# Last layer: two source blocks at a time, count rows on four row groups, clamps on two engines

## The chip, the cores and the metric

The kernel runs on one core of a Trainium2 chip. A core has a matrix engine (TensorE, PE in the profile, with its weight loads shown as PEld), three engines for elementwise work (VectorE or DVE, ScalarE or ACT, GpSimd or POOL), a queue for data movement (SyncE or SP), an on-chip memory of 128 partitions, and eight PSUM banks of 512 fp32 values a partition, into which TensorE accumulates. The metric is the time of one execution in microseconds (us).

## The reference

Four graph layers follow each other on 4096 nodes with 64 features, all over the same 4096 x 4096 adjacency matrix; each is preceded by a layer norm with a maximum at zero, and adds its result to the nodes. The change is in the last layer (and in the end of the third, which prepares an operand for it):

```python
support = input @ weight
mask = (adj != 0).astype(support.dtype)
rank = jnp.cumsum(mask, axis=1)
deg = rank[:, -1:]
k = jnp.minimum(deg, float(MAX_NEIGH))  # 100
pos = rank - (deg - k)
w = mask * jnp.where(pos > 0, DECAY ** (k - pos), 0.0)  # DECAY = 0.5
out = w @ support + bias
```

So an edge from a source column weighs 0.5 to the power of the number of edges to its right in the same row, and nothing if there are 100 or more of these.

## The kernel before

**Layout.** Sources stand in 32 blocks of 128 (NB = 32, index j), on the partitions. Destinations stand on the free axis, in groups of 512 (G), which is one PSUM bank. The transposed edge mask lies in device memory as one byte an edge and is loaded by SyncE in pieces of four source blocks (`m`, L2747, JT = 4, NQ = 8 pieces).

**The weight as a number's bits.** The kernel never computes a power. It builds, in PSUM, 128 x (100 - number of later edges) where there is an edge and something not positive where there is none or too many are later; clamped at zero and written as a 16-bit integer, this is the bit pattern of a bf16 power of two (128 is one step of its exponent). Two products make it. The triangle product (L2762) multiplies the 128 x 128 matrix `tri` with the block's mask: the diagonal gives 100 x 128 at an edge, the rest subtracts 128 for each later edge in the same block. The count-row product (L2754) adds what later blocks hold: `late` has, on 32 partitions, one count for each source block (already limited to 128), and `blk` picks row j and spreads it, times -128, over 128 partitions. It contracts over 32 partitions only, so it takes up one of TensorE's four groups of 32 rows.

**The loop.** For each quarter of the destinations (u = 0 to 3, 1024 columns, NK = 2 groups) the kernel goes over the 32 blocks. For each block: two count-row products into the two halves of one PSUM tile `pv` of two banks, two triangle products on top of these, one clamp of all 1024 columns on ScalarE (L2771) into `w3b`, and then, for the block before, two sums (L2736) of the supports `SS` times the weights into `sacc`, which are two PSUM banks held for the whole quarter. The pool `ps_v` has two `pv` tiles, four banks; `w3b` has three buffers. After the quarter the sums are copied out by ScalarE and VectorE (`ev`, L2778), turned by small products with `fold_3` (L2783), and VectorE adds the bias and the nodes (`og`, L2791 and L2792); GpSimd's queue stores the result (L2793).

**Which row groups.** `late` holds four times 32 rows for each half of the destinations, one set for each group of 512. Quarter u uses the sets (u mod 2) x 2 and the next one: two row groups at a time.

**What sets the order around it.** The layers are written as loops, and a scheduler orders the instructions of each engine ahead of time; at run time each engine goes through its own list in that order and waits on semaphores. The third layer is done in two halves of the destinations (`hf`). The groups of its second half (`layer2_group`, four serial chains over TensorE, VectorE and ScalarE: L2634, the transposes L1000, L2645, the norm, and at the end L2668 and `SS` at L2671 to L2674) therefore stand mixed with the last layer's first quarter, whose `late` is ready from the first half's end. That quarter's sums of the second half of the sources need the `SS` of these groups. At the end of each half a product (L2724) and a limit (L2725) make `late` of that half.

Of the kernel before, what the change touches and what calls it, by code (L numbers as in the profile page):

```python
# [9 lines left out]
F32 = mybir.dt.float32  # L10
BF16 = mybir.dt.bfloat16
F16 = mybir.dt.float16
F8 = mybir.dt.float8e4
I32 = mybir.dt.int32
I8 = mybir.dt.int8
I16 = mybir.dt.int16
U8 = mybir.dt.uint8
AF = mybir.ActivationFunctionType
ALU = mybir.AluOpType
AX = mybir.AxisListType  # L20
PSUM = bass.MemoryType.PSUM
# [3 lines left out]
P = 128  # L25
N = 4096
NB = N // P
D = 64
G = 512
NG = N // G  # L30
GB = G // P
JT = 4
# [803 lines left out]
def kernel(  # L836
# [24 lines left out]
    nc = tc.nc  # L861
    NH, F, O = W_sp.shape[0] + W_int.shape[0], W_sp.shape[1], W_sp.shape[2]
# [178 lines left out]
    with ExitStack() as l0:  # L1041
        lp = l0.enter_context(tc.tile_pool(name="l0", bufs=1))
# [258 lines left out]
        with ExitStack() as pa:  # L1301
            hp = pa.enter_context(tc.tile_pool(name="prep", bufs=1))
            work = pa.enter_context(tc.tile_pool(name="pwork", bufs=2))
# [47 lines left out]
            with in_order():  # L1351
                nc.vector.tensor_reduce(fsum, FT[0:F, :], AX.X, ALU.add)
                for b0 in range(0, NB, 8):
                    pw = (ps, ps2)[b0 // 8 % 2].tile([P, 8, KZ], F32, name="pst", tag="misc")
                    for b in range(8):
                        nc.tensor.matmul(
                            pw[:, b, :],
                            lhsT=FT[:, (b0 + b) * P : (b0 + b + 1) * P],
                            rhs=rhz,
                            start=True,  # L1360
                            stop=True,
# [19 lines left out]
                for g in range(HW // G):  # L1381
                    pr = (ps, ps2)[g % 2].tile([P, G], F32, name="psr", tag="misc")
                    nc.tensor.matmul(
                        pr, lhsT=srep, rhs=FT[:, g * G : (g + 1) * G], start=True, stop=True
# [27 lines left out]
                for k in range(2):  # L1412
                    pr = ps.tile([P, G], F32, name="prs", tag="misc")
                    for q in range(4):
# [3 lines left out]
                            lhsT=rs,  # L1418
                            rhs=FT[:, g * G : (g + 1) * G],
                            start=True,  # L1420
                            stop=True,
# [23 lines left out]
        with ExitStack() as ha:  # L1445
            hp = ha.enter_context(tc.tile_pool(name="heads", bufs=2))
            work = ha.enter_context(tc.tile_pool(name="hwork", bufs=1))
# [458 lines left out]
        HO2 = N // 4  # L1906
# [614 lines left out]
    def layers_fast(es, wide, *sums):  # L2521
# [75 lines left out]
        with not_before_nodes():  # L2597
# [25 lines left out]
            nc.vector.tensor_scalar(w3, w3, Q3[0:D], VAL, ALU.mult, ALU.mult)  # L2623
            fold_3 = lp.tile([P, D], F32, name="fold_3f")
            nc.vector.tensor_scalar(fold_3, fold_h, M3, 2.0**27 / VAL, ALU.mult, ALU.mult)
        late = lp.tile([P, 2, G], BF16, name="late")

        def layer2_group(b0, part, deg):

# [47 lines left out]
        with tc.tile_pool(name="ps_nacc", bufs=6, space=PSUM) as ps_acc:  # L2677
            for hf in range(2):
                accs = [ps_acc.tile([P, G], F32, name="nacc", tag="nacc") for _ in range(NS)]
                dc = ps_acc.tile([P, G], F32, name="dc", tag="nacc")  # L2680
                for q in range(NQ):
                    m = work.tile([P, JT, HW], U8, name="m2", tag="m2", bufs=3)
                    nc.sync.dma_start(m, mask_d[q][hf])
                    m8 = m.bitcast(F8)
                    for t in range(JT):
                        j = q * JT + t
                        for k in range(NS):
                            nc.tensor.matmul(  # L2688
                                accs[k],
                                lhsT=HH[:, j].rearrange("p s d -> p (s d)"),  # L2690
                                rhs=m8[:, t, k * G : (k + 1) * G],
                                start=(j == 0),
                                stop=(j == NB - 1),
                            )
                    for t in range(JT):
                        j = q * JT + t
                        for k in range(NS):
                            nc.tensor.matmul(
                                dc[k * O : (k + 1) * O, :],
                                lhsT=sel[:, j * O : (j + 1) * O],  # L2700
                                rhs=m8[:, t, k * G : (k + 1) * G],
                                start=(j == 0),
                                stop=(j == NB - 1),
                            )
                cf = work.tile([P, G], F32, name="cf", tag="cf")
                nc.vector.tensor_copy(cf, dc)
                nc.gpsimd.tensor_copy(cnt16[:, hf], cf)
                ev = work.tile([P, NS, G], F32, name="ev2", tag="ev2", bufs=1)
                for k in range(NS):
                    (nc.vector.tensor_copy if k % 2 else nc.scalar.copy)(ev[:, k, :], accs[k])  # L2710
                pd = ps.tile([P, GB, NS], F32, name="pdeg", tag="misc")
                for b in range(GB):
                    nc.tensor.matmul(  # L2713
                        pd[:, b], lhsT=cf[:, b * P : (b + 1) * P], rhs=qsel, start=True, stop=True
                    )
                deg = work.tile([P, NS, GB], F32, name="degf", tag="degf")
                nc.vector.tensor_scalar(
                    deg.rearrange("p q b -> p b q"), pd, 1.0, 1.0, ALU.add, ALU.max
                )
                nc.vector.reciprocal(deg, deg)  # L2720
                for g in range(NS):
                    layer2_group(hf * HB + g * GB, ev[:, g, :], deg[:, g, :])
                pl = ps.tile([P, G], F32, name="plate", tag="misc")
                nc.tensor.matmul(pl, lhsT=lat, rhs=cnt16[:, hf], start=True, stop=True)  # L2724
                nc.vector.tensor_scalar(late[:, hf], pl, VBITS, None, ALU.min)  # L2725


        ps_acc = es.enter_context(tc.tile_pool(name="ps_sacc", bufs=2, space=PSUM))
        ps_v = es.enter_context(tc.tile_pool(name="ps_v", bufs=2, space=PSUM))
        for u in range(4):  # L2730
            hs = slice((u % 2) * HO2, (u % 2 + 1) * HO2)
            accs = [ps_acc.tile([P, G], F32, name="sacc", tag="sacc") for _ in range(NK)]

            def add_up(j, w):
                for k in range(NK):
                    nc.tensor.matmul(  # L2736
                        accs[k],
                        lhsT=SS[:, j].rearrange("p s d -> p (s d)"),
                        rhs=w[:, k * G : (k + 1) * G].bitcast(BF16),
                        start=(j == 0),  # L2740
                        stop=(j == NB - 1),
                    )

            last = None
            for q in range(NQ):
                m = work.tile([P, JT, HO2], U8, name="m3", tag="m3", bufs=3)
                nc.sync.dma_start(m, mask_d[q][u // 2][:, :, hs])  # L2747
                for t in range(JT):
                    j = q * JT + t

                    pv = ps_v.tile([P, HO2], F32, name="pv", tag="pv")
                    for k in range(NK):
                        r = ((u % 2) * NK + k) * O
                        nc.tensor.matmul(  # L2754
                            pv[:, k * G : (k + 1) * G],
                            lhsT=blk[r : r + O, j, :],
                            rhs=late[r : r + O, u // 2, :],
                            start=True,
                            stop=False,
                        )  # L2760
                    for k in range(NK):
                        nc.tensor.matmul(  # L2762
                            pv[:, k * G : (k + 1) * G],
                            lhsT=tri,
                            rhs=m[:, t, k * G : (k + 1) * G].bitcast(F8),
                            start=False,
                            stop=True,
                        )

                    w = work.tile([P, HO2], I16, name="w3b", tag="w3b", bufs=3)  # L2770
                    nc.scalar.activation(w, pv, AF.Relu)  # L2771
                    if last is not None:
                        add_up(*last)
                    last = (j, w)
            add_up(*last)
            ev = work.tile([P, NK, G], F32, name="ev3", tag="ev3")
            for k in range(NK):
                (nc.vector.tensor_copy if k % 2 else nc.scalar.copy)(ev[:, k, :], accs[k])  # L2778
            for k in range(NK):
                b0 = (u * NK + k) * GB  # L2780
                pn = ps.tile([P, GB, D], F32, name="pn3", tag="misc")
                for b in range(GB):
                    nc.tensor.matmul(  # L2783
                        pn[:, b, :],
                        lhsT=ev[:, k, b * P : (b + 1) * P],
                        rhs=fold_3,
                        start=True,
                        stop=True,
                    )
                og = work.tile([P, GB, D], F32, name="og", tag="og")  # L2790
                nc.vector.tensor_tensor(og, pn, b3t.unsqueeze(1).to_broadcast([P, GB, D]), ALU.add)  # L2791
                nc.vector.tensor_tensor(og, og, x[:, b0 : b0 + GB, :], ALU.add)  # L2792
                nc.gpsimd.dma_start(  # L2793
                    out[b0 * P : (b0 + GB) * P, :].rearrange("(b p) f -> p b f", p=P), og
                )
# [92 lines left out]
```

## Time and profile before

| What | Value |
|---|---|
| median of 3 runs | 2041.64 us (2033.41 to 2043.93) |
| the profiled execution | 2039.13 us, of which the span from first to last instruction is 2037.1 us |
| TensorE, VectorE, ScalarE busy over the span | 89%, 75%, 72% |
| first count-row product of the last layer | at 1826.4 us |
| its four quarters end (copies `ev` start) | 1894.4, 1938.8, 1982.8, 2026.8 us |
| clamps L2771 | 128 of 1.02 us on ScalarE |

A row of a group of instructions reads: line, engine, operation, output<-input with the shapes, count, then the busy time in us and the mean of one in ns, then the idle time of its engine just ahead of it and what ended most of that. A row of the timeline reads: start, duration, engine, line, operation, and how many were merged; in brackets the idle time ahead and its releaser. A stage's row gives its bounds, its length, and each engine's busy time with the number of instructions.

### The profile page before, as it was taken

How to read it: one execution, taken by the hardware profiler on the slowest of the kernel's cores; microseconds unless marked ns; L12 is line 12 of the kernel's file. 1: busy time of each engine (PE TensorE's matmuls, PEld its weight loads, DVE VectorE, ACT ScalarE, POOL GpSimd, SP SyncE). 2: the span in 40 equal slices, each digit the busy share in tenths (PEclk: the TensorE clock that was granted, in tenths of full speed). 3: DMA queues.
4: the chain of work that ended last, by engine and by line, in shares of the span. 5: the costliest groups of instructions: out<-in, count | busy, mean ns of one | idle time of the engine just before them, and what ended most of it. 6: DMA issues, size and time to landing. Idle time of an engine off the chain costs nothing. (4 is left out here: it accounts for less than half of the span.)

```text
span 2037.1 us, 44155 instructions
## 1 busy us (share of the span) xinstructions
PE 1815.8 (89%) x19323; PEld 821.8 (40%) x19340; DVE 1530.0 (75%) x2239; ACT 1476.9 (72%) x1439; POOL 83.3 (4%) x125
## 2 busy tenths in 40 slices
PE   5889989999999999996788958999999995789998
PEld 3444445444444444443234442333333333344332
DVE  5779988998789879996989867888788788533000
ACT  2768987899689878993778847777777753227676
POOL 2000100100000000001011100000000000000000
PEclk8899999999999999997899977999999996899999
DMA  9945555434211111103686406444344334412232
GB/s 112 178 115 99 100 99 72 164 118 172 86 49 49 48 49 54 54 2 125 254 276 227 163 17 235 137 145 143 124 140 140 124 134 151 152 63 70 91 99 64
DMA packets 117016, 239.05 MB, mean 117 GB/s; under 512 B 11062, under 2 KB 84006, under 8 KB 102054
## 3 DMA queue, kind: packets, MB, share of 16 engines
q1 hardware_dynamic: 101996, 192.95, 28.1%
q0 software_dynamic: 14816, 43.18, 11.8%
q8 instruction: 153, 2.51, 0.5%
q14 instruction: 51, 0.42, 0.1%
HBM read 245.37 MB, written 49.46 MB: 145 GB/s over the span
## 5 line engine op out<-in xcount | busy, mean ns | idle before, releaser
L1205 ACT ACTIVATE st<-srow,nt 128x2048 int8<-128x2048 f32 x352 | 682.8, 1994 | 78.9 <-DVE B L1211 78.1
L1211 DVE TENSOR_TENSOR B<-st,mres 128x1024 int32<-128x1024 int32 x256 | 311.7, 1220 | 70.5 <-PE accC L1541 46.6
L1541 PE MATMUL accB<-B,ybh 128*32 128x512 fp8e4 x3072 | 340.6, 384 | 13.3 <-DVE B L1211 13.3
L1541 PE MATMUL accD<-B,ybh 128*32 128x512 fp8e4 x2048 | 303.0, 388 | 23.0 <-DVE h L1657 23.0
L1541 PEld LDWEIGHTS <-ybh 128*32 128x32 bf16 (+1 forms) x6656 | 197.4, 98 | 236.8 <-issue 74.8
L1541 PE MATMUL accC<-mres,ych 128*32 128x512 fp8e4 x2272 | 269.2, 381 | 0.0
L1541 PE MATMUL accC<-B,ycn 128*32 128x512 fp8e4 x2272 | 269.0, 381 | 0.0
L1541 PE MATMUL accL<-B,ybh 128*32 128x512 fp8e4 x1536 | 221.6, 390 | 4.6 <-DVE h L1661 4.5
L1541 PEld LDWEIGHTS <-ych 128*32 128x32 f16 x4096 | 170.2, 99 | 116.1 <-issue 11.3
L1199 DVE TENSOR_SCALAR st<-srow,nt 128x2048 uint8<-128x2048 f32 x160 | 205.4, 1284 | 2.5
L2339 PE MATMUL accj<-sg,who 128*64 128x512 f32 (+1 forms) x512 | 197.8, 616 | 5.9 <-DVE sg L2332 5.5
L2339 PE MATMUL acci<-sg,who 128*64 128x512 f32 (+1 forms) x512 | 197.8, 616 | 0.0
L2295 ACT ACTIVATE yt<-pu,consts 128x512 f32<-128x512 f32 x144 | 98.7, 687 | 98.7 <-PE pu L2294 98.6
L2284 ACT ACTIVATE sg<-pl,rb 128x512 f32<-128x512 f32 x256 | 160.9, 679 | 8.2 <-PE pl L2279 5.2
L2771 ACT ACTIVATE w3b<-pv 128x1024 int16<-128x1024 f32 x128 | 131.0, 1024 | 42.4 <-PE pv L2762 41.2
L1205 ACT ACTIVATE st<-srowo,nto 128x1024 int8<-128x1024 f32 x128 | 138.3, 1138 | 25.0 <-DVE B L1211 24.9
L1541 PE MATMUL accC<-C,ych 128*32 128x512 fp8e4 x1824 | 149.3, 393 | 0.8 <-DVE C L1219 0.8
L955 DVE SCALAR_TENSOR_TENSOR raw<-raw 128x2048 f32<-128x2048 f32 x64 | 146.1, 2282 | 3.3 <-DMA raw<-in_adj_dram 3.3
L1219 DVE TENSOR_TENSOR C<-B,mres 128x1024 int32<-128x1024 int32 x114 | 139.5, 1225 | 3.6
L1541 PEld LDWEIGHTS <-ycn 128*32 128x32 f16 x2272 | 108.4, 97 | 62.7 <-issue 1.9
L2332 DVE SCALAR_TENSOR_TENSOR sg<-pf,sg 128x512 f32<-128x512 f32 x112 | 72.1, 685 | 38.9 <-PE pf L2329 38.9
L2778 DVE COPY ev<-sacc 128x512 f32<-128x512 f32 x4 | 2.8, 691 | 124.8 <-PE sacc L2736 124.8
(497 smaller groups left out, 2756.4 us busy)
## 6 DMA issues: line engine op xcount, KB each, us to landing
raw<-in_adj_dram SPq DMA_DIRECT2D x64, 1024.0 KB, 6.0
mo<-edges SPq DMA_DIRECT2D x32, 512.0 KB, 4.9
noedge<-nmo POOLq DMA_DIRECT2D x32, 512.0 KB, 4.3
nm<-noedge SPq DMA_DIRECT2D x64, 256.0 KB, 3.1
m<-edges SPq DMA_DIRECT2D x16, 1024.0 KB, 4.8
m<-edges SPq DMA_DIRECT2D x32, 512.0 KB, 3.8
srow<-srow_d SPq DMA_DIRECT2D x15, 1024.0 KB, 6.7
mres<-in_adj_dram POOLq DMA_DIRECT2D x8, 1024.0 KB, 35.4
```

Source lines behind the costliest of these rows:

```text
L955: nc.vector.scalar_tensor_tensor(raw, raw, 0.0, raw, ALU.is_gt, ALU.not_equal, accum_out=bad[:, c : c + 1])
L1199: nc.vector.tensor_scalar(st[:, i, :].bitcast(U8), srow, negs[:, i : i + 1], EDGE, ALU.is_gt, ALU.mult)
L1205: nc.scalar.activation(st[:, i, :], srow, AF.Sign, bias=negs[:, i : i + 1], scale=-1.0)
L1211: nc.vector.tensor_tensor(B.bitcast(I32), st.bitcast(I32), edges.bitcast(I32), ALU.bitwise_and)
L1219: nc.vector.tensor_tensor(C.bitcast(I32), B.bitcast(I32), edges.bitcast(I32), ALU.bitwise_xor)
L1541: ins = nc.tensor.matmul(acc[k * O : (k + 1) * O, :], lhsT=values, rhs=moving(k), start=start, stop=stop,)
L2284: nc.scalar.activation(sg[:, b0 + k, :], pl, AF.Sigmoid, bias=rb[:, j : j + 1], scale=1.0)
L2295: nc.scalar.activation(far[gi, gj][:, b, :], pu, AF.Sigmoid, bias=nb_t, scale=2.0 * DIST_K / (DIST_S * DIST_S),)
L2332: nc.vector.scalar_tensor_tensor(v[:, t, :], pf, F_K3, v[:, t, :], ALU.add, ALU.mult)
L2339: nc.tensor.matmul(acc[r : r + n, :], lhsT=XQ[:, src, cols], rhs=w, start=start, stop=stop)
L2771: nc.scalar.activation(w, pv, AF.Relu)
L2778: (nc.vector.tensor_copy if k % 2 else nc.scalar.copy)(ev[:, k, :], accs[k])
```

## The change

Two source blocks are now taken together, in four steps:

- `pv` is no longer one tile of two banks for a block, but four tiles of one bank each for a pair of blocks (block i = 0 or 1, group k = 0 or 1). The pool has four such tiles, the same four banks.
- The four count-row products of a pair stand one after another, each on another group of 32 rows. For the second block they use the other two row groups, so the counts must also lie there: `late_x` is `late` with its halves of 64 partitions exchanged, written by two more VectorE operations at the end of each half of the third layer.
- Four triangle products follow, then the four sums of the pair before. `w3b` holds two blocks in each of its three buffers.
- The clamp is done for each bank by itself, by ScalarE for k = 0 and by VectorE for k = 1: two of 512 columns on each engine for a pair.

```diff
-        late = lp.tile([P, 2, G], BF16, name="late")
+        late, late_x = (lp.tile([P, 2, G], BF16, name=n) for n in ("late", "late_x"))
...
                 nc.vector.tensor_scalar(late[:, hf], pl, VBITS, None, ALU.min)
+                for lo, hi in ((slice(0, D), slice(D, P)), (slice(D, P), slice(0, D))):
+                    nc.vector.tensor_scalar(late_x[lo, hf], pl[hi], VBITS, None, ALU.min)
...
-        ps_v = es.enter_context(tc.tile_pool(name="ps_v", bufs=2, space=PSUM))
+        ps_v = es.enter_context(tc.tile_pool(name="ps_v", bufs=4, space=PSUM))
...
-            def add_up(j, w):
-                for k in range(NK):
-                    nc.tensor.matmul(
-                        accs[k],
-                        lhsT=SS[:, j].rearrange("p s d -> p (s d)"),
-                        rhs=w[:, k * G : (k + 1) * G].bitcast(BF16),
-                        start=(j == 0),
-                        stop=(j == NB - 1),
-                    )
+            def add_up(j0, w):
+                for i, j in enumerate(range(j0, j0 + 2)):
+                    for k in range(NK):
+                        nc.tensor.matmul(
+                            accs[k],
+                            lhsT=SS[:, j].rearrange("p s d -> p (s d)"),
+                            rhs=w[:, i, k * G : (k + 1) * G].bitcast(BF16),
+                            start=(j == 0),
+                            stop=(j == NB - 1),
+                        )
...
-                for t in range(JT):
-                    j = q * JT + t
-
-                    pv = ps_v.tile([P, HO2], F32, name="pv", tag="pv")
-                    for k in range(NK):
-                        r = ((u % 2) * NK + k) * O
+                for t0 in range(0, JT, 2):
+                    j0 = q * JT + t0
+                    both = [(i, k) for i in range(2) for k in range(NK)]
+                    pvs = {ik: ps_v.tile([P, G], F32, name="pv", tag="pv") for ik in both}
+                    for i, k in both:
+                        r = ((u + i) % 2 * NK + k) * O
                         nc.tensor.matmul(
-                            pv[:, k * G : (k + 1) * G],
-                            lhsT=blk[r : r + O, j, :],
-                            rhs=late[r : r + O, u // 2, :],
+                            pvs[i, k],
+                            lhsT=blk[r : r + O, j0 + i, :],
+                            rhs=(late, late_x)[i][r : r + O, u // 2, :],
                             start=True,
                             stop=False,
                         )
-                    for k in range(NK):
+                    for i, k in both:
                         nc.tensor.matmul(
-                            pv[:, k * G : (k + 1) * G],
+                            pvs[i, k],
                             lhsT=tri,
-                            rhs=m[:, t, k * G : (k + 1) * G].bitcast(F8),
+                            rhs=m[:, t0 + i, k * G : (k + 1) * G].bitcast(F8),
                             start=False,
                             stop=True,
                         )
 
-                    w = work.tile([P, HO2], I16, name="w3b", tag="w3b", bufs=3)
-                    nc.scalar.activation(w, pv, AF.Relu)
+                    w = work.tile([P, 2, HO2], I16, name="w3b", tag="w3b", bufs=3)
+                    for i, k in both:
+                        wk = w[:, i, k * G : (k + 1) * G]
+                        if k:
+                            nc.vector.tensor_scalar(wk, pvs[i, k], 0.0, None, ALU.max)
+                        else:
+                            nc.scalar.activation(wk, pvs[i, k], AF.Relu)
                     if last is not None:
                         add_up(*last)
-                    last = (j, w)
+                    last = (j0, w)
```

## The prediction

> **What bounds the kernel now.** I read the page first. Its groups give the clamp of the last layer as a ScalarE job of 1024 ns that mostly waits for TensorE, while VectorE does nothing in that layer but wait for sums:
>
> ```profile
> L2771 ACT ACTIVATE w3b<-pv 128x1024 int16<-128x1024 f32 x128 | 131.0, 1024 | 42.4 <-PE pv L2762 41.2
> L2778 DVE COPY ev<-sacc 128x512 f32<-128x512 f32 x4 | 2.8, 691 | 124.8 <-PE sacc L2736 124.8
> ```
>
> Then the busy time by stage. The first line names the columns, the second is the third quarter of the destinations (u=2):
>
> ```profile
> core 0: us, PE busy (x) PEld busy (x) DVE busy (x) ACT busy (x) POOL busy (x), PEclk, DMA share, GB/s
> 1937.60:1980.60 43.00, 42.45 (x201) 14.34 (x204) 2.21 (x5) 32.58 (x33) 1.50 (x2) 1.00 0.34 104
> ```
>
> TensorE is busy 99% of it at the full clock, ScalarE 76%, VectorE 5%. So TensorE's order of work sets the pace. The timeline shows it, one source block after another:
>
> ```profile
> 1911.17 0.39 PE L2754 MATMUL pv<-late,LDf 32*128 32x512 bf16 x2
> ...
> 1911.49 0.61 PE L2762 MATMUL pv<-m,tri 128*128 128x512 fp8e4 x2
> ...
> 1911.93 0.59 PE L2736 MATMUL sacc<-w3b,XAf 128*128 128x512 bf16 x2
> 1912.19 1.02 ACT L2771 ACTIVATE w3b<-pv 128x1024 int16<-128x1024 f32 x1 [0.31 <-PE pv L2762]
> ...
> 1912.46 0.39 PE L2754 MATMUL pv<-late,LDf 32*128 32x512 bf16 x2
> ...
> 1912.78 0.61 PE L2762 MATMUL pv<-m,tri 128*128 128x512 fp8e4 x2
> ...
> 1913.27 0.59 PE L2736 MATMUL sacc<-w3b,XAf 128*128 128x512 bf16 x2
> ```
>
> The step to the triangle products is 0.32 us, to the sums 0.44 or 0.49, back to the count rows 0.53 or 0.52: 1.31 us a block, 2.62 for two. Inside a kind the second product starts about 0.215 after the first (0.59 for two sums of 0.377 each); two count-row products start together (0.39 for both, 0.385 for one). So three changes of kind cost about 0.1, 0.03 and 0.1 over streaming.
>
> The chain of waits has a second bound. Until 1891.6 the layer-2 groups of the second half still run between the blocks, one serial chain of 14.8 us a group (its transposes of h start at 1842.84, 1857.63, 1872.41, 1887.33), and the sums of the first quarter cannot finish before its end. Two more pieces of timeline:
>
> ```profile
> 1884.18 1.02 ACT L2771 ACTIVATE w3b<-pv 128x1024 int16<-128x1024 f32 x1 [0.27 <-PE pv L2762]
> ...
> 1885.26 0.39 PE L2754 MATMUL pv<-late,LDf 32*128 32x512 bf16 x2 [0.25 <-ACT w3b L2771]
> ...
> 1885.58 0.11 PEld L2762 LDWEIGHTS <-tri 128*128 128x128 bf16 x2 [0.23 <-issue]
> ...
> 1890.09 0.69 DVE L2725 TENSOR_SCALAR late<-plate 128x512 bf16<-128x512 f32 x1 [2.81 <-PE plate L2724]
> ...
> 1891.61 0.60 PEld L2736 LDWEIGHTS <-XAf 128*128 128x128 f16 x4 [1.86 <-ACT XAf L2674]
> ```
>
> ```profile
> 1817.82 1.28 DVE L2710 COPY ev<-nacc 128x512 f32<-128x512 f32 x2
> ```
>
> A count-row product that waits for a clamp starts 0.05 after its end (1885.20 to 1885.26), and the triangle 0.32 later. VectorE takes 0.69 for 512 columns out of PSUM, 1.28 for two in a row.
>
> **What the Trainium skill says.** "TensorEngine Tiling (Array Packing)", Key Properties: changing the tiling mode drains TensorE; the trace agrees (0.32 into the triangle against 0.215). "TensorE: Matmul & The Clock Gate", Part 3: four 32-row products of 512 columns ran 3.07 times as fast as in a row, starts about 4 ns apart; this trace shows two at once, never four. The first page, Gotcha 1: different row tiles may not write one PSUM bank, which four single-bank tiles obey. "VectorE: DVE Perf Modes", Why PSUM operands drop a tier: fp32 from PSUM goes at the plain rate; the 0.69 fits.
>
> **The change part by part**, with time 0 at the first triangle product of a pair of blocks.
>
> 1. TensorE alone. Four count rows at once 0.32, four triangles 3x0.215+0.25 = 0.895, four sums 3x0.215+0.31 = 0.955: 2.17 a pair against 2.62. One set of mode changes is gone.
>
> 2. The new wait. All four PSUM tiles belong to the current pair, so no tile is free ahead: the fourth count row of the next pair waits for VectorE's second clamp of this one, and behind it on TensorE wait the four triangles and all that follows. Triangle two starts at 0.215; VectorE starts 0.49 after such a start (last sum at 2026.60, its copy at 2027.09) and needs 1.28 for both clamps: 1.985. Count row at 2.035, triangle at 2.355. ScalarE's pair (a 512-column copy is 0.59, L1001) ends near 1.65 and hides; the sums hide behind it too. So the period is 2.36, not 2.17: 0.26 gained a pair. The clamp to int16 on VectorE is in no row. Bounds: 0.60 each where TensorE sets the pace (2.17), 0.9 if the conversion costs a third more (2.8). I take 0.69, the TENSOR_SCALAR that writes bf16, as it is the same form.
>
> 3. The quarters' ends. Before, a quarter takes 44.0 (count rows at 1942.28 and 1986.26): 32x1.31 and 2.0 for the output products L2783. After, the changed program's order has the last pair's four sums, three count rows, then the output products, which wait for the copies (start of last sum 2.41, VectorE's copy to 3.6), then the fourth count row and the triangles: output products from 3.3 to 5.3, triangle at 5.6. The next pair's rows meet VectorE late, as four og operations (0.42, 0.42, 0.75) stand ahead of its clamps. Followed to the third pair I get 10.3 against 3x2.36 = 7.1: a cost of 3.2. A quarter is 16x2.36+3.2 = 41.0, a gain of 3.0; two such quarters 6.0.
>
> 4. The tail: from the triangle of the last two blocks to the end of the last sum 2023.29 to 2026.98, 3.7; after 2.4+0.4 = 2.8. Gain 0.9. The copies, og and the output DMA behind it stay.
>
> 5. Around the first quarter's end. The three w3b buffers now hold two blocks each, so TensorE has the triangles of four blocks of u=1 done before the last group's transpose, instead of one. From the end of the chain: eight sums at the slow clock (0.43 each, as now), four count rows, output products 2.0, sums of pair 0, triangles of pair 2, sums of pair 1: count row of block 6 at +9.1, against 1899.35+3x1.31-1891.6 = +11.7. Gain 2.6. The remaining 13 pairs of u=1 give 13x0.26 = 3.4.
>
> 6. The layer-2 chain, a loss. The first quarter's own pairs gain nothing, since the chain covers them; what counts is its end. late_x is four VectorE operations of 64x512; the ScalarE copy of 64x512 costs as much as one of 128x512 (0.58, 0.59), so 0.69 each, 1.28 a pair. The first pair stands behind lo and ahead of the degree operations L2717; those wait for the products L2713 anyway, which now wait for lo. TensorE then also has a sum that waits for a ScalarE clamp ahead of L2634. Followed through, the first group ends about 1.5 later. In each later group VectorE's queue holds clamps between the chain's operations: one between nrm and the reciprocal (hidden by the square root on ScalarE), one ahead of zt (+0.35), one ahead of h and one ahead of ln_var (+0.8 together); ScalarE's shorter clamps give back 0.75 (the two waits for a 1024-column clamp, 0.5 and 0.45, go, and the copy cT is earlier). Net +0.4 for two groups, +1.2 for the last, whose queue holds two more clamps. Sum 3.5, bounded by 0 and 8.
>
> The m3 loads keep number, size and queue; they land in 3.8 and are asked for two quads (over 9 us) ahead: nothing. The second late_x pair runs at the stall that ends at 1891.6: nothing.
>
> Sum: 2.6+3.4+6.0+0.9-3.5 = 9.4. The profiled execution took 2039.13 (span 2037.1): 2029.7. The median of the three runs is 2041.64, so 2032.2; I say 2032.
>
> **Rivals.**
>
> *TensorE is the bound after all.* VectorE's clamps follow closer, the period is 2.17 and the layer-2 chain hardly suffers. For it: only 0.19 a pair separates the two bounds. Against: 0.69 is measured on this kind of operation. 45 pairs x 0.19 = 8.6 and 2 back from the chain: 2021.
>
> *The layer-2 chain eats the gain.* VectorE was 32% busy in the first quarter (21.87 of 68.3 us) and gets 32 clamps, 20 us more, in a queue that can't reorder. In the changed order some five chain operations a group have a clamp just ahead; if each waits a whole 0.6, that is 2.8 a group and 11 in all rather than 3.5: 2040.
>
> *Slower: the four row groups don't run at once.* Place: every pair, as the count rows start. If they go one after another, TensorE's block is 0.32+3x0.215 = 0.965, its period 2.815, over the old 2.62. Against the 2.36 this costs 45x0.455 = 20.5: 2052.5. It decides from a block of about 0.72, where the period of 2.57 has used up the sum. For it: nothing in this trace runs four; against: the skill's 3.07 and the two that start together. A VectorE clamp of 0.9 would end in the same place.
>
> **How the numbers follow.** About 0.5%, 10 us, is what a measurement of this kernel can tell from no change; the three runs span that. The forecast has 0.50, its own range 2026 to 2038, of which 0.24 lies below 2031.4 and 0.26 within. TensorE bound 0.24, all faster. Chain eats it 0.12, within. Not at once, or slow clamps, 0.14, of which 0.13 slower and 0.01 within. So faster 0.48, same 0.39, slower 0.13. The range reaches from the TensorE bound at 2021 past the chain case to 2043.
>
> **What would show it.** Right: VectorE's w3b group x128 near 690 ns with ScalarE's x128 near 600; groups of four count rows 2.36 apart in u=1 to 3; their wait put down to DVE w3b; four late_x; the last chain ending near 1895. Wrong: count rows of a group starting 0.2 apart; spacing 2.17 with no wait for w3b (first rival); transposes of h more than 16.5 apart (second); a VectorE clamp over 0.8; a stall at each quarter's end over 5 us.

## The result, and the profile after

The changed kernel takes 2024.40 us (median of six runs, 2020.27 to 2031.64) beside 2040.91 for the kernel before (six runs, 2033.41 to 2043.93). The ratio is 0.9926, 95% interval 0.9907 to 0.9945: faster by 0.74%, some 15 us, where 9.4 had been forecast. Two more sets of runs of the same kernel gave 0.9926 and 0.9932.

The page's groups, in the columns of before: the two clamp groups are there in the sizes forecast, 594 ns on ScalarE and 685 on VectorE.

```profile
L2779 ACT ACTIVATE w3b<-pv 128x512 int16<-128x512 f32 x128 | 70.5, 594 | 80.2 <-issue 47.9
L2777 DVE TENSOR_SCALAR w3b<-pv 128x512 int16<-128x512 f32 x128 | 83.5, 685 | 51.5 <-issue 39.2
```

Busy time of the changed kernel inside the third quarter of the destinations (the stretch of before was 1937.60 to 1980.60):

```profile
core 0: us, PE busy (x) PEld busy (x) DVE busy (x) ACT busy (x) POOL busy (x), PEclk, DMA share, GB/s
1941.00:1977.00 36.00, 35.91 (x182) 12.12 (x180) 20.38 (x33) 17.26 (x32) 1.50 (x2) 1.00 0.35 110
```

VectorE went from 5% to 57% and ScalarE from 76% to 48%. TensorE still reads as busy nearly all the time, but this view hides short waits: the record of a count-row product lasts 0.385 us from its start, so a wait of the next one that is shorter than that leaves no gap between the two records. The timeline of a pair of blocks tells it apart:

```profile
1909.14 1.04 PE L2765 MATMUL pv<-m,tri 128*128 128x512 fp8e4 x4
1909.62 1.08 ACT L2779 ACTIVATE w3b<-pv 128x512 int16<-128x512 f32 x2 [1.19 <-issue]
...
1909.86 1.29 DVE L2777 TENSOR_SCALAR w3b<-pv 128x512 int16<-128x512 f32 x2 [1.07 <-PE pv L2765]
1910.02 1.03 PE L2739 MATMUL sacc<-w3b,XAf 128*128 128x512 bf16 x4
1910.97 0.10 PEld L2757 LDWEIGHTS <-LDf 32*128 32x128 bf16 x4 [0.42 <-issue]
1910.98 0.39 PE L2757 MATMUL pv<-late,LDf 32*128 32x512 bf16 x2
1910.98 0.59 PE L2757 MATMUL pv<-late_x,LDf 32*128 32x512 bf16 x2
...
1911.51 1.04 PE L2765 MATMUL pv<-m,tri 128*128 128x512 fp8e4 x4
```

The two `late` products take 0.39 together. The `late_x` pair takes 0.59, as its second product, the fourth count row, starts 0.2 later than the first. VectorE's two clamps end at 1909.86 + 1.29 = 1911.15; with step 2's 0.05 to the count row and 0.32 on to the triangles that gives 1911.52, and they start at 1911.51. That is step 2 of the prediction; the period from triangle to triangle is 2.37 here and 2.345 later (count rows at 2008.61, 2010.96, 2013.31, 2015.65).

The boundary from the second to the third quarter:

```profile
1934.96 1.04 PE L2765 MATMUL pv<-m,tri 128*128 128x512 fp8e4 x4
...
1935.84 1.89 PE L2739 MATMUL sacc<-w3b,XAf 128*128 128x512 bf16 x8
...
1937.66 0.39 PE L2757 MATMUL pv<-late,LDf 32*128 32x512 bf16 x2
...
1938.19 2.00 PE L2791 MATMUL pn<-fold_3f,ev 128*128 128x64 f32 x16
...
1940.43 1.04 PE L2765 MATMUL pv<-m,tri 128*128 128x512 fp8e4 x4
...
1945.05 1.04 PE L2765 MATMUL pv<-m,tri 128*128 128x512 fp8e4 x4
```

From the last pair's triangles the next are at +5.47 (5.6 forecast) and the third pair's at +10.09 (10.3). A quarter, from one ScalarE copy of the sums to the next, is 40.6 (1937.55 to 2018.75 over two) against 44.0.

To compare traces I take the layer from the start of the transposes of h of the last first-half group (tile `tr` from `h`) to the end of the last copy of the sums. It is 206.7 before (1821.12 to 2027.78) and 195.5 after (1824.19 to 2019.66).

### The profile page after: what moved, and what is told of

Same layout as the page of the kernel before. It is cut to its first block, busy times and chain, and to the rows that moved or that the text cites. A ratio compares the mean times of both kernels' runs of the same rounds, so it can differ in the third digit from the quotient of the medians.

```text
span 2029.8 us, 44281 instructions
## 1 busy us (share of the span) xinstructions
PE 1806.8 (89%) x19340; PEld 822.9 (41%) x19340; DVE 1614.2 (80%) x2371; ACT 1417.7 (70%) x1439; POOL 83.2 (4%) x125
## 5 line engine op out<-in xcount | busy, mean ns | idle before, releaser
L1541 PE MATMUL accB<-B,ybh 128*32 128x512 fp8e4 x3072 | 340.6, 385 | 13.3 <-DVE B L1211 13.3
L2779 ACT ACTIVATE w3b<-pv 128x512 int16<-128x512 f32 x128 | 70.5, 594 | 80.2 <-issue 47.9
L2777 DVE TENSOR_SCALAR w3b<-pv 128x512 int16<-128x512 f32 x128 | 83.5, 685 | 51.5 <-issue 39.2
```

Source lines behind the costliest of these rows:

```text
L1541: ins = nc.tensor.matmul(acc[k * O : (k + 1) * O, :], lhsT=values, rhs=moving(k), start=start, stop=stop,)
L2777: nc.vector.tensor_scalar(wk, pvs[i, k], 0.0, None, ALU.max)
L2779: nc.scalar.activation(wk, pvs[i, k], AF.Relu)
```

## The experiments

Ratios are to the kernel before on the same chip, whose medians beside the experiments were 2040.3 to 2042.7.

### The changed kernel again

No edit.

> The changed kernel once more, beside the variants. Every theory: ratio to the kernel before near 0.993, pairs of blocks 2.345 us apart in the last two quarters.

Measured: 2023.91, ratio 0.9926 (0.9900 to 0.9953). The period and the quarters repeat. The layer is 196.4.

### Who clamps which half

```diff
-                        if k:
+                        if not k:
                             nc.vector.tensor_scalar(wk, pvs[i, k], 0.0, None, ALU.max)
```

VectorE takes the first half of each block, tiles one and three, instead of two and four.

> The two clamp engines exchanged: VectorE takes k = 0 (first and third bank), ScalarE k = 1 (second and fourth). If the fourth count row's wait for VectorE's second clamp sets the period (the theory): VectorE now starts one triangle (0.215) earlier and frees the third bank at about 1.80, ScalarE (1.08 for two) the fourth at about 1.83, both before TensorE is through with the sums at 1.87; the period falls from 2.345 to TensorE's own 2.17 to 2.20, 45 pairs give about 7 us, ratio near 0.989. If TensorE's own work is the 2.345 (rival): no change.

Measured: 2019.11 (2015.53 to 2025.06), ratio 0.9892 (0.9863 to 0.9922). The timeline of one pair, from the second trace of this version (told below; the first has the same spacing):

```profile
1986.80 0.39 PE L2757 MATMUL pv<-late,LDf 32*128 32x512 bf16 x2
1986.80 0.39 PE L2757 MATMUL pv<-late_x,LDf 32*128 32x512 bf16 x2
...
1987.12 1.04 PE L2765 MATMUL pv<-m,tri 128*128 128x512 fp8e4 x4
1987.61 1.29 DVE L2777 TENSOR_SCALAR w3b<-pv 128x512 int16<-128x512 f32 x2 [0.87 <-ACT w3b L2779]
...
1988.00 1.03 PE L2739 MATMUL sacc<-w3b,XAf 128*128 128x512 bf16 x4
...
1988.95 0.39 PE L2757 MATMUL pv<-late,LDf 32*128 32x512 bf16 x2
...
1989.28 1.04 PE L2765 MATMUL pv<-m,tri 128*128 128x512 fp8e4 x4
```

VectorE now starts 0.49 after the first triangle instead of 0.72, all four count rows start within 0.01 and take 0.39, and the period is 2.16: the TensorE bound of the first rival, 2.17. Nothing but the order of the clamps differs, so it was VectorE's second clamp that held the changed kernel at 2.35. The clamps still only just fit: VectorE's end at 1988.90 (1987.61 + 1.29), and the next count rows start at 1988.95, just when TensorE has issued its sums. The two limits lie level now.

### Two row groups instead of four

```diff
-    r = ((u + i) % 2 * NK + k) * O
+    r = (u % 2 * NK + k) * O
...
-    rhs=(late, late_x)[i][r : r + O, u // 2, :],
+    rhs=late[r : r + O, u // 2, :],
```

with `late_x` gone. The rest is the changed kernel.

> Pairs of blocks as in the change, but all count rows on the two row groups of before, from late alone; late_x is gone. If VectorE's clamp sets the period: the count rows of the second block start 0.215 after the first block's, mostly inside the wait that is there anyway; period about 2.41, 45 pairs lose 3 us, and the missing late_x gives back at most 1.4 us at the start. Total within 3 us of the changed kernel. If the four row groups are what the change lives on (rival): 2.345 + 0.215 = 2.56, a loss of about 10 us, most of the gain.

Measured: 2028.34 (2021.76 to 2034.66), ratio 0.9942 (0.9923 to 0.9961), period 2.37, layer 195.4. In the trace the pair is longer by only 0.02 without four row groups: what the groups save, the wait for VectorE takes back. The timed median is 4.4 us above that of the changed kernel beside it, where the theory had at most 3; the two intervals overlap, and the trace, which is of the shortest of the twelve executions, does not show where these 4.4 would be. The same edit on the swapped version, where the count rows don't wait for a clamp:

> The version with the clamps swapped (VectorE takes the first half of each block), but all four count rows of a pair on the two row groups of before and no late_x. Theory: with the clamps out of the way TensorE sets the period, and now the row groups show: two more steps of 0.215 in the count rows, 2.16 + 0.22 = 2.38 a pair, some 45 x 0.22 = 9 to 10 us over the swapped version, less 1 us for late_x gone from the layer-2 chain: near 2027. Rival (the row groups are worth nothing, as the pair of runs without the swap suggests): period 2.16 to 2.2, time at the swapped version's 2019.

Measured: 2023.75 (2022.47 to 2029.39), ratio 0.9928 (0.9899 to 0.9956).

```profile
1990.67 0.60 PE L2755 MATMUL pv<-late,LDf 32*128 32x512 bf16 x4
...
1991.21 1.04 PE L2763 MATMUL pv<-m,tri 128*128 128x512 fp8e4 x4
...
1993.05 0.60 PE L2755 MATMUL pv<-late,LDf 32*128 32x512 bf16 x4
```

Four count rows on two groups take 0.60 instead of 0.39 and the period is 2.37 to 2.38. The layer is 195.3 against 186.4, 8.9 us: the full price of the row groups, and the theory's 9 to 10. The timed difference, 4.6, is smaller than that of the traces, and the time lies 3 under the 2027 of the theory; that stays open. The saving of one part is only there once the other limit is lifted.

### The clamps shared, the blocks not paired

The order of before (one block at a time), with two single-bank tiles a block and one clamp on each engine:

```diff
-    pv = ps_v.tile([P, HO2], F32, name="pv", tag="pv")
+    pvs = [ps_v.tile([P, G], F32, name="pv", tag="pv") for _ in range(NK)]
...
-    nc.scalar.activation(w, pv, AF.Relu)
+    for k in range(NK):
+        wk = w[:, k * G : (k + 1) * G]
+        if k:
+            nc.vector.tensor_scalar(wk, pvs[k], 0.0, None, ALU.max)
+        else:
+            nc.scalar.activation(wk, pvs[k], AF.Relu)
```

> The kernel before, one block at a time, with only the single-bank tiles and the clamps shared by the two engines. Theory: TensorE's order with its three changes of kind for each block is untouched, so a block stays at 1.31 us (2.62 for two), a quarter at 44 us; the total within 4 us of before, either way through the layer-2 chain. Rival (the clamp's length was what TensorE waited for): a block falls below 1.25 us and the total gains more than 8 us.

Measured: 2049.36 (2044.62 to 2053.50), ratio 1.0043 (1.0027 to 1.0058): slower by 8.9, where the theory had 4 at most. A block takes 1.29 instead of 1.31, and the third and fourth quarters 43.4 and 43.3 instead of 44.0. So sharing the clamps in the old order is worth 0.6 us a quarter, and is not by itself the gain of the change. The loss that the trace shows lies earlier. The five transposes of h of the layer-2 chain span 72.9 and the second quarter takes 49.0 instead of 44.4. Ahead of the chain's last group TensorE has nothing left to do (argued: the three `w3b` buffers are full) and stands idle for 3.03 us, till `h` is there:

```profile
1888.40 1.03 PE L1000 MATMUL tr<-ident,h 128*64 128x128 f32 x4 [3.03 <-DVE h L986]
```

Four transposes, 0.60 in the changed kernel, take 1.03, as TensorE's clock is at half speed from 1886 to 1910:

```profile
1868.00:1886.00 18.00, 14.93 (x63) 7.92 (x62) 8.91 (x24) 6.35 (x14) 0.00 (x0) 0.81 0.10 30
1886.00:1910.00 24.00, 19.15 (x58) 9.00 (x60) 7.97 (x16) 5.69 (x12) 1.55 (x2) 0.51 0.12 40
```

(The column ahead of the DMA share is the granted clock.) Were the clamps in VectorE's queue, among the chain's operations, the cause? The same version with both clamps of a block on ScalarE in the first quarter, `if u and k:`:

> The order of before (one block at a time), single-bank rank tiles and shared clamps, but in the first quarter both clamps of a block on ScalarE. The version with them shared everywhere was 8.8 us slower than before, its layer-2 chain 7.3 longer. Theory: VectorE's clamps in the chain are that loss; the chain's intervals return to within 1 us of before's 21.7, 14.8, 14.8, 14.9 and the time to 2041 to 2043. Rival: the loss is in the split tiles (TensorE released twice a block, two ScalarE operations of 0.6 for one of 1.02): it stays above 2046.

Measured: 2039.84 (2034.14 to 2054.07), ratio 1.0002 (0.9984 to 1.0021). The time fell as the theory said, by 9.5. Its reason shows in the intervals between the five transposes, though not in their sum, which goes from 72.9 to 72.2 (the 72.9 were 6.7 over that of before, not the 7.3 of the text above). With the clamps shared they are 23.24, 16.84, 16.16 and 16.70; with those of the first quarter on ScalarE 25.89, 15.33, 15.32 and 15.70; in the kernel before 21.72, 14.79, 14.78 and 14.92. The second and third pass at TensorE's full clock in all three traces. There the shared clamps had added 3.43 us, and the edit takes 2.35 of them away: that much is VectorE's clamps in the chain. The 1.08 that stays is left to the rival, the split tiles, which no run tests alone. The first interval is longer, not shorter, with 20.5 us of it at half the clock instead of 10.2; the clock is taken up below.

The trace is of the longest of the fourteen executions (span 2052.3), with the second quarter at 48.3. So how the 9.5 us of the medians are made up beyond the chain stays open.

### All clamps on ScalarE

```diff
-                        if k:
+                        if False:
```

> The changed kernel with all four clamps of a pair on ScalarE. Theory: the loop of a pair closes over the clamps: first clamp 0.48 after the first triangle, four of 0.51 to 0.6 in a row, 0.05 to the fourth count row, 0.32 to the triangle: 2.9 (2.8 to 3.2) a pair instead of 2.35, more than the 2.62 of before; 45 pairs x 0.55 = 25 less about 3 that the chain gets back: near 2046, slower than before. Rival: ScalarE's clamps hide behind TensorE's work and the period stays at 2.35 to 2.6: at most 2036.

Measured: 2049.07 (2043.31 to 2054.50), ratio 1.0040 (1.0020 to 1.0060).

```profile
2016.03 1.04 PE L2765 MATMUL pv<-m,tri 128*128 128x512 fp8e4 x4
2016.52 2.06 ACT L2779 ACTIVATE w3b<-pv 128x512 int16<-128x512 f32 x4 [0.84 <-PE pv L2765]
...
2018.14 0.86 PE L2757 MATMUL pv<-late_x,LDf 32*128 32x512 bf16 x2
...
2018.94 1.04 PE L2765 MATMUL pv<-m,tri 128*128 128x512 fp8e4 x4
```

0.49 to the first clamp, 2.06 for four, 0.05 and 0.31 to the triangles: 2.91, as worked out. Paired blocks without sharing are slower than the old order. Neither pairing nor sharing gains alone; together they do.

### What lengthens the layer-2 chain

In the first traces of the two kernels the chain (five transposes of h) had grown from 66.2 to 69.7, just the 3.5 of step 6. I tried to take it back, on the swapped version, by all four clamps on ScalarE in the first quarter:

```diff
-                        if not k:
+                        if u and not k:
```

> The version with the clamps swapped, but in the first quarter (u=0), which runs beside the layer-2 chain, all four clamps of a pair are on ScalarE; from u=1 on they are shared. Theory: the chain grew because clamps stand in VectorE's queue between its operations; ScalarE then has 4 x 0.6 = 2.4 a pair where it had 2.05 before the change, so the chain's intervals go back to about 22 to 23 for the first group (late_x stays) and 14.8 for the others: 2 to 3 us off, near 2016.5. Rival: the chain waits for ScalarE as much as for VectorE, and the ten operations a group that it has there now meet more clamps: the intervals stay or grow (16 or more), time 2019 or above.

Measured: 2019.48 (2015.09 to 2026.48), ratio 0.9909 (0.9879 to 0.9939). The intervals are 24.42, 15.97, 14.61 and 14.41, in all 69.4: the sum is not shorter than with the clamps shared (23.55, 14.72, 14.72, 15.78; 68.8), and the time is the same. But theory and rival each hold in one group. The last interval falls by 1.4, to less than the 14.92 of before, so what had lengthened it is VectorE's clamps. The second grows by 1.25, to the 16 of the rival. Both pass at the full clock, and the changed kernel with all its clamps on ScalarE repeats them (15.97 and 14.55). Two of VectorE's clamps in the last group of the swapped version, from its second trace:

```profile
1886.00 0.17 DVE L972 TENSOR_SCALAR ln_mean<-ln_mean 128x4 f32<-128x4 f32 x1
1886.08 0.68 DVE L2777 TENSOR_SCALAR w3b<-pv 128x512 int16<-128x512 f32 x1
1886.68 0.41 DVE L973 TENSOR_TENSOR h<-x,ln_mean 128x256 f32<-128x256 f32 x1
...
1888.69 0.29 ACT L983 ACTIVATE ln_var<-ln_var,consts 128x4 f32<-128x4 f32 x1
1888.84 0.69 DVE L2777 TENSOR_SCALAR w3b<-pv 128x512 int16<-128x512 f32 x1 [0.22 <-PE pv L2765]
1889.45 0.17 DVE L985 RECIPROCAL ln_var<-ln_var 128x4 f32<-128x4 f32 x1
```

`h` (L973) starts 0.51 after the end of the operation ahead of it in the chain and the reciprocal (L985) 0.47, where they start 0.10 and 0.03 after it with the clamps on ScalarE. That is 0.85 of the 1.4. In that version, in turn, ScalarE's `ln_sq` (L977) of the second interval starts 0.42 after `h`, behind a clamp, instead of 0.04.

Next, the first quarter in the order of before, single blocks with 1024-column clamps on ScalarE, and pairs from the second on:

```diff
+    if u == 0:
+        pv = ps_v0.tile([P, HO2], F32, name="pv", tag="pv")
...
+        nc.scalar.activation(w[:, 0, :], pv, AF.Relu)
```

> The version with the clamps swapped, but the first quarter (u=0) works as before: one block at a time, one ScalarE clamp of 1024 columns, two two-bank rank tiles; pairs with shared clamps from u=1 on (late_x stays). Neither late_x nor the engine of the clamps explained the longer layer-2 chain. Theory: it is the order of work on TensorE, which has a pair's triangles and a sum ahead of the chain's next products (pnf starts 1.9 us later in the first group): with single blocks the five transposes of h are again 66 to 67 apart in all, not 68.8 to 69.7. The lookahead into u=1 is smaller, which costs about 2.6 again, so the time stays within 3 us of the swapped version's 2019. Rival: the chain keeps 68.5 or more, its length is set elsewhere, and the time is 2021 or more.

Measured: 2024.05 (2021.47 to 2032.72), ratio 0.9929 (0.9906 to 0.9953): 22.92, 14.79, 14.97, 14.93, in all 67.6, between the two theories. Its last interval is that of before, which fits, as the clamps of the first quarter have left VectorE's queue here too. The time is 5 above that of the swapped version: from the last transposes of h to the second quarter's first copy it takes 47.8 instead of 40.4, where the smaller lookahead was to cost 2.6; TensorE's clock is at half speed for 10.2 us from these transposes on. The first interval moves from trace to trace in a way that the edits don't explain, and for that the kernel before was traced again:

> The kernel before once more, unchanged, for a second trace of it. In the two traces at hand the last layer, from the transposes of h of the last first-half group to the last copy of sums, is 206.7 us before and 195.5 after: 11.2 gained, while the timed medians differ by 16. If the first trace of before is a short one in that layer, this one shows 208 to 212 there; if the layer is again 206 to 207, the other 5 us come from the part of the kernel ahead of it, where the two kernels have the same work, and the ratio here shows how far two sets of runs of one kernel differ: 1.000 within 0.003.

Measured: 2038.84, ratio 0.9993 (0.9979 to 1.0006). The layer is 211.2 this time, not 206.7, and of the 4.6 more, 4.7 are in the first interval of the chain: 26.45 against 21.72, then 14.79, 14.78, 14.92 as before. The same stretch of the two traces, first that of the prediction, then the new one; the transposes of h start it at 1821.12 and 1821.18:

```profile
1824.00:1832.00 8.00, 7.41 (x29) 5.15 (x30) 2.15 (x6) 1.72 (x3) 0.19 (x1) 0.50 0.00 1
1832.00:1844.00 12.00, 11.64 (x54) 4.50 (x54) 4.08 (x12) 9.07 (x14) 0.21 (x1) 0.92 0.17 49
```

```profile
1824.00:1832.00 8.00, 7.35 (x29) 5.09 (x30) 2.21 (x6) 1.66 (x3) 0.13 (x1) 0.50 0.00 1
1832.00:1844.00 12.00, 11.64 (x33) 4.13 (x33) 3.06 (x9) 5.18 (x8) 0.27 (x1) 0.50 0.14 44
```

In the first trace the clock comes back to full speed near 1834, in the second near 1844. TensorE is as busy in both, but gets through 54 products in one and 33 in the other. The kernel and its work are the same, and from 1824 to 1832 the two traces read alike, with 29 products each. Summed over the granted clock in steps of 1 us, the stretch is worth 10.2 us at half speed in the first trace and 20.5 in the second; over all traces of this case such stretches of this layer are 3.4, 10.2, 13.6, 17.1, 20.5 and, in two pieces of 6.8 and 23.9, 30.7: multiples of 3.4. "TensorE: Matmul & The Clock Gate", Part 1 of the Trainium skill, has a free-running window of 3413 ns after which the clock falls to half or comes back; the step of these lengths agrees. It says that the clock comes back after at least one busy window; here TensorE reads as busy for 11.64 of 12 us and stays at half speed, so either more than one was needed, or what this view counts as busy is not what the clock goes by.

In the two traces of before, 10.2 us more of half speed come with 4.7 more of time, or 0.46 for 1; between the changed kernel's own traces it is 0.26 (24.35 at 13.6, 25.23 at 17.1). What follows is an estimate with 0.46. At 13.6 before's first interval would be 23.3, where the changed kernel's first trace has 24.3; at 17.1 it would be 24.9, where its other two have 25.2. So the change adds some 0.3 to 1.0 to the first group, not the 2.6 that the first pair of traces shows. At the same 13.6, taking `late_x` away saves 0.5 (24.34 to 23.85) in the changed kernel and 0.6 (23.55 to 22.96) in the swapped one. And the version with the first quarter's clamps on ScalarE had 17.1 where the swapped one had 13.6: at 0.46 that hides 1.6, so that the clamps on VectorE may cost the chain up to 1.0 net (68.8 less 67.8), where the theory had 2 to 3.

### The swapped version beside the changed one

Both once more, on one chip, without edits.

> The version with the clamps swapped once more, beside the changed kernel on the same chip, for a second trace and a closer comparison. Theory: 0.19 less a pair in the 45 pairs that no chain covers, 8 to 9 us in the last layer: ratio to before near 0.989, 6 to 9 us under the changed kernel. Rival: the 5 us between their first runs were spread, and the two agree within 2 us. The length of the half-speed stretch of TensorE's clock after the first-half groups, 10 to 20 us in the traces so far, is expected to differ again between these two traces with no regard to the version.

> The changed kernel a third time, on the same chip as the swapped version. Theory: 2023 to 2026, last layer 195 to 197 from the transposes of h of the last first-half group to the last copy of sums (before: 206.7 and 211.2). Rival: its layer varies by 5 as that of before does, 193 to 200.

Measured: swapped 2018.65 (2011.94 to 2025.51), ratio 0.9890 (0.9861 to 0.9919); changed 2025.19 (2023.40 to 2038.08), ratio 0.9932 (0.9911 to 0.9953). The layer is 186.4 in both traces of the swapped version and 195.5, 196.4 and 196.4 in the three of the changed one, so it holds better than that of before. The swapped version beats both kernels: by 6.5 us here and 4.8 in the first runs, where the layers differ by 9 to 10. The half-speed stretch came out at 13.6 in both traces of the swapped version and at 17.1 in the last two of the changed one. That is up to 1.6 us of the difference at 0.46 each, and may belong to the version after all.

## Why the prediction was right, and where not

**Steps 1 and 2, the period.** Right, with their mechanism. 2.345 to 2.37 for 2.36 forecast, the fourth count row is what waits, and VectorE's second clamp is what it waits for: with the clamps swapped the wait is gone and the period falls to 2.16, the 2.17 of step 1. The int16 clamp on VectorE, which no row of before had, took 0.685 where 0.69 was chosen, and 1.29 for two where 1.28 was. The prediction didn't see that the order of the two engines decides between its forecast and its first rival.

**Step 3, the quarters' ends.** Right: 40.6 for 41.0 a quarter, 6.8 us for 6.0 in two.

**Step 4, the tail.** Right: last triangles at 2016.17, last sum's end at 2018.93, 2.76 for 2.8.

**Step 5, around the first quarter's end.** The mechanism was right, the size too small. From the chain's end (1898.13) the count rows of block 6 come at 1906.40, +8.3 for +9.1; before it was 11.5 (1903.30, from 1891.84), so 3.2 for 2.6. The eight sums alone took 3.0 (to 1901.14) where 8 x 0.43 = 3.4 was counted. The pairs that follow are 2.34 apart (28.05 for twelve). From the last transposes of h to the second quarter's first copy it is 43.7 in all three traces of the changed kernel against 51.5 and 51.3: 7.7 for 6.0. In the first pair of traces it is 1.8 more than forecast: 0.6 in this walk, 0.6 in the twelve pairs (31.74 to 28.05, where 12 x 0.26 = 3.1 was counted), 0.4 in the last pair, which gains at its end as step 4 has it for the tail, and 0.3 in the chain's steps behind these transposes (4.51 to 4.25).

**Step 6, the chain.** The direction was right, the split wrong, and that the first two traces gave just its 3.5 (66.2 to 69.7) was chance, as they differ in the clock. The middle groups gained 0.07 each (14.79 to 14.72) where 0.4 each was to be lost: the list of what each clamp costs and gives back there is the working that failed. That ScalarE's shorter clamps gave back all that was lost was argued and isn't shown; that ScalarE's part in a group is worth over 1 us is (the 1.25 above). The last group lost 1.0 for 1.2, and to VectorE's clamps, as forecast: without them it takes 14.4. The first lost some 0.3 to 1.0 for 1.5. In all some 1.2 to 1.9 for 3.5.

**The sum.** 7.7 + 6.8, less 1.2 to 1.9: 12.6 to 13.3 for 9.4. Behind the last transposes of h it is 14.5, with step 4's gain inside, where 2.6 + 3.4 + 6.0 + 0.9 = 12.9 was forecast. So 1.6 of what was missed lies here, and as much or more in the chain's loss, counted too large. The layers say the same: the mean of two traces before is 208.9, of three after 196.1, 12.9 gained. The prediction also took one trace as the base, and that one had a half-speed stretch of 10.2, the shortest seen in its place. The remaining 2 to 4 us of the timed 15 to 17 lie within the interval of the ratio (11 to 19); the start of the layer alone, behind the same work, lies anywhere from 1814 to 1828 in these traces. No cause is shown for them.

**The rivals.** The TensorE bound didn't come with the change as written, but with one condition turned round. That the chain eats the gain: no, it took at most 2 us. That the row groups don't run at once: no, four start within 0.01 and take 0.39 together where one takes 0.385. The forecast's own range, 2026 to 2038, was missed by 1.6; the result fell between it and the first rival, and the wider range held it.

## What to carry to other kernels

When a software pipeline has no spare tile, list which engine releases each tile and start the slower engine on the tile that is ready first: in the traces here, turning one condition round was worth as much as four row groups, and until it was done the row groups were worth next to nothing. Changes that share one limit are to be tried together, since neither pairing nor sharing gained alone. Compare a serial chain group by group: here its sum hid that moving the clamps took 1.4 from one group and put 1.25 on another. And look at the granted clock before a difference between two traces is explained: here 4.7 us of a serial chain came with it in two executions of one kernel.

## What the runs showed of the hardware

- Two VectorE clamps of 128x512 out of PSUM, one after the other, take 1.29 (0.685 the mean of one), two on ScalarE 1.08 and four 2.06 (0.594 and 0.602): in a row, a ScalarE one costs about 0.49.
- Four 32-row products of 512 columns on four row groups start within 0.01 us and take 0.39 together; on two row groups four take 0.60.
- The half-speed stretches of TensorE's clock come in multiples of 3.4 us and last up to 23.9 in one piece in this layer. TensorE reads as busy for 77 to 97% of those of 6.8 and more. Their length differs between two executions of one kernel.
- The busy share hides short waits: TensorE reads 99.7% busy (35.91 of 36.00) in the changed kernel, which still had 0.19 a pair to give.
